# Row means from a ninth router column, variances from ACT's Square, and the states' sum as one bf16 product of exact pieces

## The chip, the core and the metric

The kernel runs on one core of a Trainium2 chip. The core has five engines with queues of their own: TensorE (PE; its weight loads are shown as PEld), VectorE (DVE), ScalarE (ACT), GpSimd (POOL) and SyncE (SP, which here only starts transfers). An engine works its queue in order, and semaphores make one engine wait for another. The metric is the device time in microseconds of one execution; the median of three runs of the kernel before is 476.83 us (476.71 to 477.4).

## The reference

One layer over 4096 tokens of width 256: a Mamba-like mixer with a residual and a layer norm, then a router that gives each token to one of eight feed-forward experts, again with a residual and a layer norm.

```python
xz = input_tensor @ W_in                       # 256 -> 1024
conv_in, gated = xz[..., :512], xz[..., 512:]
convolved = silu(causal_conv4(conv_in) + conv_b)
x_dbl = convolved @ W_x                        # 512 -> 33
delta = softplus(x_dbl[..., :1])
Bm, Cm = x_dbl[..., 1:17], x_dbl[..., 17:]
deltaA, deltaBx = exp(delta * -exp(A_log)), delta * Bm * convolved[..., :16]
# per token: h = dA * h + dBx ;  ys = sum(h * c) over the 16 states
skip_out = ys[..., None] + convolved * D_param
x1 = layernorm(x + (skip_out * silu(gated)) @ W_out)
e = argmax(x1 @ Wr.T + br)
out = layernorm(x1 + relu(x1 @ W1[e].T + b1[e]) @ W2[e].T + b2[e])
```

A layer norm takes the mean and the variance of each row of 256 and gives `(x - m) / sqrt(v + 1e-5)`. `ys` is one number per token, added to all 512 channels.

## The kernel before

The 4096 tokens go through the mixer in eight blocks of 512 (`NB`, `TB`). The loop over `k` (L1047) is a software pipeline: in one round it projects block k, works on the states of block k - 1, gates and projects out block k - 2, and ranks the tokens of block k - 3 for the experts. From round 6 on, quarters of expert blocks (`expert(n)`) are woven in, and after the loop the last rounds and the remaining expert blocks follow. There are 32 blocks of up to 128 tokens of one expert; from about 290 us on only these are left.

The order on TensorE is written out by hand (`manual_schedule` for PE, L120), and is that of the calls in the loop. The other engines' orders are set by a planner that goes by estimated times; so a change of one operation can move others of the same engine. An engine still works in order whatever the planner chose.

The pieces of a round that matter here, in TensorE's order:

- `project(k, c)`, c from 0 to 7 (L744): 128 channels by 512 tokens in fp32, two products of 128 rows each, which TensorE runs as four instructions, into one of three PSUM banks `mm`. ACT takes them out: channels 0 to 511 twice (a copy `xc`, L761, and `acc`, L763, the first tap of the convolution), the rest through Silu into `sg` (L759). VectorE does the other three taps (L723), ACT the Silu of the result, `cv` (L772).
- `gate(k - 2)` (L865), after `project(k, 0)`: the states times C, `hC`, are summed over the 16 states and spread over 128 partitions by a product with ones, `py` (L872). In fp32 this is done in two halves of 256 tokens, on rows 0 to 15 and 32 to 47 of the array, which run side by side into two banks. VectorE then forms `cv * D + py` (L879), eight times 128x256, and VectorE and POOL multiply by `sg` (L884).
- `gauge(k - 1)` and `gauge_out(k - 1)` (L780, L794): the 33 columns of `W_x`, turned so that tokens lie on partitions, and the step sizes `delta` by a series on VectorE, into `sr`.
- `project_out(k - 2, j)`, j from 0 to 3 (L916), spread over the round: 128 tokens by 256 + 8 columns, four products. The eight columns beside W_out are W_out times the router's weights (`router_behind`, L484), and `look` and `look_out` (L886, L901) add x times the router's weights, so that the router's sums come with the rows. The router's weights have their mean over the 256 features taken out first (`router_weights`, L470), so the logits need only the scale of the layer norm. VectorE adds the product to `xb` (L924) and takes the mean and the variance with its statistics instructions (L928, L929). After j = 3 ACT takes the square root (L934), VectorE the reciprocal and the offset `nma` (L935, L937), and ACT writes the normalized rows `x1` (L940), which a transfer stores for the experts.
- `scan(k - 1)` (L841), late in the round: `sr` is turned so that states lie on partitions (`pt`, L846), ACT forms the decay `dA` (L848), VectorE the input `dBx` (L850), the scan over 512 tokens (L852) and `hC` (L860). `hC` is then taken by `gate` of the next round. `sg` of projection 6 and the copies `rparts` (L912) stand in front of `dA` on ACT.
- `choose`, `rank`, `place` (L948, L974, L1014): argmax, rank of each token in its expert's list, and the lists as 0/1 products `pz` (L1019), which VectorE adds to `lists` (L1023).

ACT holds one set of function tables at a time; Silu, Exp and Sqrt are in different ones here, and a change shows in the profile as an ACT_TABLE_LOAD of 1283 ns.

Of the kernel before, what the change touches and what calls it, by code (L numbers as in the profile page):

```python
# [47 lines left out]
P = 128  # L48
# [37 lines left out]

O2 = DC * FF
# [12 lines left out]
def mamba_moe(  # L100
# [36 lines left out]
    def load(i):  # L137

        xTb = a2.tile([P, DC, TB], F32, tag="xTb", name=f"xTb{i}")
        at = slice(i * TB, (i + 1) * TB)  # L140
        if i:
            nc.sync.dma_start(xTb, xT[:, at].rearrange("(c p) t -> p c t", p=P))

        xb = a2.tile([P, JT, D + NE], F32, tag="xb", name=f"xb{i}")
        st[i] = {"xTb": xTb, "xb": xb}
# [29 lines left out]
    nc.vector.memset(wr, 0.0)  # L175
    nc.sync.dma_start(wr[:, :, 0:NE], WrT.rearrange("(c p) e -> p c e", p=P))
# [5 lines left out]
    wout = const.tile([P, CC, D + NE], F32, name="wout")  # L182
# [60 lines left out]
    nc.gpsimd.memset(sr, 0.0)  # L243
    ones8 = const.tile([P, NE], F32, name="ones8")
# [239 lines left out]
    def router_behind(half):  # L484
        po = bank("tr", f"pwo{half}", 2)
        pov = po[:, 0 : CC * NE].rearrange("p (c e) -> p c e", e=NE)
        cs = slice(half * CC // 2, (half + 1) * CC // 2)
        for c in range(CC)[cs]:
            for dc in range(DC):
                nc.tensor.matmul(  # L490
                    pov[:, c, :], lhsT=woutT[:, dc, c * P : (c + 1) * P], rhs=wr[:, dc, 0:NE],
                    start=(dc == 0), stop=(dc == DC - 1),
                )
        nc.scalar.copy(wout[:, cs, D : D + NE], pov[:, cs, :])
# [346 lines left out]
    def scan(i):  # L841
# [15 lines left out]
        hC = a2.tile([Q + NS, TB // 2], F32, tag="hC", name=f"hC{i}", bufs=1)  # L857
        for g in range(2):
            at = slice(g * TB // 2, (g + 1) * TB // 2)
            nc.vector.tensor_tensor(  # L860
                hC[g * Q : g * Q + NS, :], pt[RC : RC + NS, at], h[:, at], ALU.mult
            )
        s_["h"], s_["hC"] = h, hC

    def gate(i):  # L865
# [3 lines left out]
        pys = [bank("o", f"py{i}_{g}") for g in range(2)]  # L869
        for g, py in enumerate(pys):  # L870
            at = slice(g * Q, g * Q + NS)
            nc.tensor.matmul(  # L872
                py[:, 0 : TB // 2], lhsT=ones[at, :], rhs=st[i]["hC"][at, :], start=True,
                stop=True, tile_position=(g * Q, 0),
            )
        for c in range(CC):
            for g, py in enumerate(pys):
                at = slice(g * TB // 2, (g + 1) * TB // 2)
                nc.vector.scalar_tensor_tensor(  # L879
                    cv[:, c, at], cv[:, c, at], dp[:, c : c + 1], py[:, 0 : TB // 2],  # L880
                    ALU.mult, ALU.add,
                )
# [18 lines left out]
    def look_out(i):  # L901
# [7 lines left out]
        beside = st[i]["xb"][:, :, D : D + NE].rearrange("p (h s) e -> p h s e", s=2)  # L909
        parts = a2.tile([P, 2, DC, 2, NE], F32, tag="rparts", name=f"rparts{i}", bufs=1)  # L910
        for s in range(2):
            nc.scalar.copy(parts[:, s], pfv[:, s, :, :, 0:NE])  # L912
# [3 lines left out]
    def project_out(i, j):  # L916
        s_, sg, xb = st[i], st[i]["sg"], st[i]["xb"]
        po = bank("o", f"po{i}_{j}")
        for c in range(CC):
            nc.tensor.matmul(  # L920
                po[:, 0 : D + NE], lhsT=sg[:, c, j * P : (j + 1) * P], rhs=wout[:, c, :],
                start=(c == 0), stop=(c == CC - 1),
            )
        nc.vector.tensor_tensor(xb[:, j, :], po[:, 0 : D + NE], xb[:, j, :], ALU.add)  # L924
        if j == 0:
            s_["mv"] = a2.tile([P, JT, 2], F32, tag="mva", name=f"mva{i}")
        sta = a2.tile([P, 6], F32, tag="sta", name=f"sta{i}_{j}")
        nc.vector.bn_stats(sta, xb[:, j, 0:D])  # L928
        nc.vector.bn_aggr(s_["mv"][:, j, :], sta)  # L929
        if j < JT - 1:  # L930
            return
        mv = s_["mv"]
        sd = s_["sd"] = a2.tile([P, JT], F32, tag="sda", name=f"sda{i}")
        nc.scalar.activation(sd, mv[:, :, 1], AF.Sqrt, bias=eps)  # L934
        nc.vector.reciprocal(sd, sd)  # L935
        nm = a2.tile([P, JT], F32, tag="nma", name=f"nma{i}")
        nc.vector.scalar_tensor_tensor(nm, mv[:, :, 0], -1.0, sd, ALU.mult, ALU.mult)  # L937
# [269 lines left out]
```

## Time and profile before

| | |
|---|---|
| median of three runs | 476.83 us (476.71 to 477.4) |
| the profiled execution | 479.7 us, span 478.0 us |
| granted TensorE clock, mean | 0.993 |
| TensorE busy | 466.2 us, 98% of the span |
| weight loads | 350.1 us |
| VectorE busy | 340.4 us, 1120 instructions |
| ACT busy | 223.4 us, 453 instructions |
| POOL busy | 185.5 us, 194 instructions |
| VectorE in 97.5 to 125.0 us (one round) | 24.98 of 27.50 us |
| ACT in the same round | 21.65 us |

The page is one profiled execution. It gives busy times and their course over the span in 40 slices, in tenths. A group of instructions stands as line, engine, operation, out<-in, shapes, count, then busy time and mean duration, then the idle time of the engine in front of them and what ended it. Matmuls are pipelined, and the ends shown are modelled: a group of four fp32 projections of 512 columns shows 1.88 us, while the next one starts 1.72 us after it. So the starts tell how long TensorE's stream needs.

### The profile page before, as it was taken

Reading aid. Unit: us, or ns where it says so; the run is one execution under the profiler, and the core shown is the slowest. Engines: PE = TensorE matmul, PEld = TensorE weight load, DVE = VectorE, ACT = ScalarE, POOL = GpSimd, SP = SyncE. Lnnn points to the kernel's source line nnn. Section 1 sums busy time; section 2 is a strip of 40 time slices with the busy share of each in tenths; the row PEclk is TensorE's granted clock in tenths of the full one; section 3 lists DMA queues with packets and bytes.
Section 4 is the critical chain, followed back from the end, with each engine's and each line's share of the span. In section 5 each row is a group of like instructions: output and inputs, shape, how many; then the busy total and the mean of one; then the engine's idle time right before and its main releaser. Section 6 shows DMA issues by size and latency. Waiting matters only on the chain. (4 is left out here: it accounts for less than half of the span.)

```text
span 478.0 us, 7559 instructions
## 1 busy us (share of the span) xinstructions
PE 466.2 (98%) x2606; PEld 350.1 (73%) x2606; DVE 340.4 (71%) x1120; ACT 223.4 (47%) x453; POOL 185.5 (39%) x194
## 2 busy tenths in 40 slices
PE   8999999999999999999999999999999999999994
PEld 6444554645455566677788999999989898989884
DVE  1687959899898997986998978755446565645453
ACT  3776767886896877584625131212212121212111
POOL 2001203442418372450433423435445456654541
PEclk9998999999999999999999999999999999999998
DMA  8401012040124945250766759799997279977910
GB/s 237 166 1 45 0 42 91 1 132 0 47 87 149 431 159 188 110 199 18 271 242 225 270 209 366 260 368 350 359 347 277 60 253 345 313 247 245 353 44 22
DMA packets 23401, 89.98 MB, mean 188 GB/s; under 512 B 4914, under 2 KB 14909, under 8 KB 19650
## 3 DMA queue, kind: packets, MB, share of 16 engines
q0 software_dynamic: 8752, 74.71, 42.7%
q1 hardware_dynamic: 13650, 14.50, 9.3%
q8 instruction: 21, 0.34, 0.3%
q10 hardware_dynamic: 960, 0.27, 0.3%
q14 instruction: 18, 0.15, 0.1%
HBM read 87.78 MB, written 9.43 MB: 203 GB/s over the span
## 5 line engine op out<-in xcount | busy, mean ns | idle before, releaser
L744 PE MATMUL pm<-xTb,win 128*128 128x512 f32 (+1 forms) x264 | 122.5, 598 | 0.0
L587 PEld LDWEIGHTS ph<-xgT,we 128*128 128x128 f32 x864 | 100.8, 192 | 5.5 <-DVE r L637 1.3
L587 PE MATMUL ph<-xgT,we 128*128 128x128 f32 x864 | 103.0, 276 | 0.0
L612 PE MATMUL pe<-we,hT 128*128 128x256 f32 x432 | 98.9, 380 | 0.0
L612 PEld LDWEIGHTS pe<-we,hT 128*128 128x128 f32 x432 | 79.7, 190 | 10.0 <-DVE lg L960 0.3
L723 DVE SCALAR_TENSOR_TENSOR acc<-xc,cw,acc 128x512 f32<-128x512 f32 x96 | 72.6, 777 | 15.7 <-DMA wx<-in_W_x 8.6
L744 PEld LDWEIGHTS pm<-xTb,win 128*128 128x128 f32 x264 | 49.2, 195 | 45.5 <-issue 40.8
L262 ACT ACTIVATE sdm<-mvm,eps 128x1 f32<-128x1 f32 x32 | 9.4, 294 | 122.6 <-DVE mvm L260 116.8
L522 POOL DMA_INDIRECT we<-in_experts,widx x32 | 33.6, 1049 | 85.0 <-DVE r L637 24.9
L920 PE MATMUL po<-wout,sg 128*128 128x264 f32 x256 | 64.1, 392 | 1.0 <-DVE sg L884 0.9
L884 POOL TENSOR_TENSOR sg<-cv,sg 128x512 f32<-128x512 f32 x22 | 32.7, 1492 | 59.6 <-DVE cv L879 46.1
L920 PEld LDWEIGHTS po<-wout,sg 128*128 128x128 f32 x256 | 46.1, 190 | 11.0 <-issue 2.9
L650 POOL DMA_INDIRECT out<-y,tidx x32 | 32.9, 1027 | 38.5 <-DVE y L264 30.5
L598 DVE TENSOR_SCALAR hT<-ph,we 128x128 f32<-128x128 f32 x108 | 31.3, 341 | 20.7 <-PE ph L587 20.6
L637 DVE TENSOR_TENSOR r<-pe,xs 128x256 f32<-128x256 f32 x32 | 13.5, 422 | 43.9 <-PE pe L612 43.8
L504 POOL DMA_INDIRECT xg<-x1d,tidx x32 | 31.9, 998 | 29.7 <-DVE xd L810 7.5
L596 ACT ACTIVATE hT<-ph,we 128x128 f32<-128x128 f32 x108 | 30.8, 368 | 23.2 <-PE ph L587 20.7
L1008 POOL TENSOR_SCALAR rowh<-lrow,row,code 128x256 f16<-128x256 bf16 x20 | 26.0, 1307 | 27.9 <-DVE row L1000 26.7
L879 DVE SCALAR_TENSOR_TENSOR cv<-cv,dp,py 128x256 f32<-128x256 f32 x64 | 28.5, 469 | 3.4 <-PE py L872 3.4
L759 ACT ACTIVATE sg<-pm 128x512 f32<-128x512 f32 x32 | 19.1, 596 | 19.5 <-PE pm L744 17.0
L761 ACT COPY xc<-pm 128x512 f32<-128x512 f32 x32 | 18.6, 582 | 19.1 <-PE pm L744 18.8
L763 ACT ACTIVATE acc<-pm,cb,cw 128x512 f32<-128x512 f32 x32 | 25.1, 784 | 0.0
(219 smaller groups left out, 604.4 us busy)
## 6 DMA issues: line engine op xcount, KB each, us to landing
xb<-in_x SPq DMA_DIRECT2D x8, 512.0 KB, 6.1
x1d<-x SPq DMA_DIRECT2D x8, 512.0 KB, 4.8
xTb<-in_xT SPq DMA_DIRECT2D x7, 512.0 KB, 3.3
win<-in_W_in SPq DMA_DIRECT2D x1, 512.0 KB, 5.2
we<-in_W_outT SPq DMA_DIRECT2D x1, 512.0 KB, 5.9
wout<-in_W_out SPq DMA_DIRECT2D x1, 512.0 KB, 6.9
we<-in_experts,widx POOLq DMA_INDIRECT x32, 10.3
xg<-x1d,tidx POOLq DMA_INDIRECT x32, 6.6
```

Source lines behind the costliest of these rows:

```text
L504: nc.gpsimd.indirect_dma_start(out=to, out_offset=None, in_=x1d[0:rows, :], in_offset=bass.IndirectOffsetOnAxis(ap=at, axis=0),)
L522: nc.gpsimd.indirect_dma_start(out=wes[n][:, :], out_offset=None, in_=experts, in_offset=bass.IndirectOffsetOnAxis(ap=weights[n], axis=0), ...
L587: nc.tensor.matmul(ph[:, n * w : (n + 1) * w], lhsT=we[:, at : at + P], rhs=xgT[:, dc * w : (dc + 1) * w], start=(dc == 0), stop=(dc == DC ...
L596: nc.scalar.activation(hT[:, fc, :], ph[:, n * w : (n + 1) * w], AF.Relu, bias=bias)
L598: last[b] = nc.vector.tensor_scalar(hT[:, fc, :], ph[:, n * w : (n + 1) * w], bias, 0.0, ALU.add, ALU.max)
L612: nc.tensor.matmul(py[:, 0:D], lhsT=hT[:, fc, 0:P], rhs=out_weights(fc), start=(fc == 0), stop=(fc == FC - 1),)
L650: moved = nc.gpsimd.indirect_dma_start(out=out, out_offset=bass.IndirectOffsetOnAxis(ap=at, axis=0), in_=rows, in_offset=None, bounds_chec ...
L723: nc.vector.scalar_tensor_tensor(acc, xc[:, c, k : k + TB], cw[:, c, k : k + 1], acc, ALU.mult, ALU.add)
L744: nc.tensor.matmul(banks[c][:, at], lhsT=win[:, dc, c * P : (c + 1) * P], rhs=xTb[:, dc, at], start=(dc == 0), stop=(dc == DC - 1),)
L879: nc.vector.scalar_tensor_tensor(cv[:, c, at], cv[:, c, at], dp[:, c : c + 1], py[:, 0 : TB // 2], ALU.mult, ALU.add,)
L884: eng.tensor_tensor(sg[:, c, :], cv[:, c, :], sg[:, c, :], ALU.mult)
L920: nc.tensor.matmul(po[:, 0 : D + NE], lhsT=sg[:, c, j * P : (j + 1) * P], rhs=wout[:, c, :], start=(c == 0), stop=(c == CC - 1),)
```

## The change

Three edits.

The router's columns become nine: the ninth column of `wr` is set to -1/256, so that the ninth column beside W_out, and the ninth sum of `look`, give minus the mean of the row. With it the statistics instructions go. The squares of the row less its mean come from ACT's Square, with the ninth column as bias and the accumulator as output; Sqrt then scales their sum by 1/256. The offset is the ninth column times the reciprocal.

The product of the states is cut into bf16 pieces. VectorE multiplies the states and C into rows 0 to 15 of `parts_`, which is cleared once. It then subtracts from these their upper half-words, read as bf16, and writes the rest to rows 32 to 47, and the same once more to rows 64 to 79. The upper half-words of all 128 rows, every second bf16 of the tile, are the moving operand of one bf16 product with ones, of 512 columns, into one bank.

The gate's update is then four operations of 128x512 and no longer eight of 128x256.

```diff
+NM = NE + 1
-        xb = a2.tile([P, JT, D + NE], F32, tag="xb", name=f"xb{i}")
+        xb = a2.tile([P, JT, D + NM], F32, tag="xb", name=f"xb{i}")
     nc.vector.memset(wr, 0.0)
+    nc.vector.memset(wr[:, :, NE:NM], -1.0 / D)
-    wout = const.tile([P, CC, D + NE], F32, name="wout")
+    wout = const.tile([P, CC, D + NM], F32, name="wout")
+    parts_ = const.tile([P, TB], F32, name="parts_")
+    nc.gpsimd.memset(parts_, 0.0)
...
                 nc.tensor.matmul(
-                    pov[:, c, :], lhsT=woutT[:, dc, c * P : (c + 1) * P], rhs=wr[:, dc, 0:NE],
+                    pov[:, c, :], lhsT=woutT[:, dc, c * P : (c + 1) * P], rhs=wr[:, dc, 0:NM],
                     start=(dc == 0), stop=(dc == DC - 1),
                 )
-        nc.scalar.copy(wout[:, cs, D : D + NE], pov[:, cs, :])
+        nc.scalar.copy(wout[:, cs, D : D + NM], pov[:, cs, :])
...
-        hC = a2.tile([Q + NS, TB // 2], F32, tag="hC", name=f"hC{i}", bufs=1)
-        for g in range(2):
-            at = slice(g * TB // 2, (g + 1) * TB // 2)
+        s_["h"] = h
+        nc.vector.tensor_tensor(parts_[0:NS, :], pt[RC : RC + NS, :], h, ALU.mult)
+        for n in range(2):
+            this = slice(n * Q, n * Q + NS)
             nc.vector.tensor_tensor(
-                hC[g * Q : g * Q + NS, :], pt[RC : RC + NS, at], h[:, at], ALU.mult
-            )
-        s_["h"], s_["hC"] = h, hC
+                parts_[(n + 1) * Q : (n + 1) * Q + NS, :], parts_[this, :], upper(this),
+                ALU.subtract,
+            )
+
+    def upper(rows):
+        return parts_[rows, :].bitcast(BF16).rearrange("p (t two) -> p t two", two=2)[:, :, 1]
...
-        pys = [bank("o", f"py{i}_{g}") for g in range(2)]
-        for g, py in enumerate(pys):
-            at = slice(g * Q, g * Q + NS)
-            nc.tensor.matmul(
-                py[:, 0 : TB // 2], lhsT=ones[at, :], rhs=st[i]["hC"][at, :], start=True,
-                stop=True, tile_position=(g * Q, 0),
-            )
+        py = bank("o", f"py{i}")
+        nc.tensor.matmul(py, lhsT=oneb, rhs=upper(slice(0, P)), start=True, stop=True)
         for c in range(CC):
-            for g, py in enumerate(pys):
-                at = slice(g * TB // 2, (g + 1) * TB // 2)
-                nc.vector.scalar_tensor_tensor(
-                    cv[:, c, at], cv[:, c, at], dp[:, c : c + 1], py[:, 0 : TB // 2],
-                    ALU.mult, ALU.add,
-                )
+            nc.vector.scalar_tensor_tensor(
+                cv[:, c, :], cv[:, c, :], dp[:, c : c + 1], py, ALU.mult, ALU.add
+            )
...
-                po[:, 0 : D + NE], lhsT=sg[:, c, j * P : (j + 1) * P], rhs=wout[:, c, :],
+                po[:, 0 : D + NM], lhsT=sg[:, c, j * P : (j + 1) * P], rhs=wout[:, c, :],
...
-            s_["mv"] = a2.tile([P, JT, 2], F32, tag="mva", name=f"mva{i}")
-        sta = a2.tile([P, 6], F32, tag="sta", name=f"sta{i}_{j}")
-        nc.vector.bn_stats(sta, xb[:, j, 0:D])
-        nc.vector.bn_aggr(s_["mv"][:, j, :], sta)
+            s_["sq"] = a2.tile([P, JT], F32, tag="sqa", name=f"sqa{i}")
+        squares = a2.tile([P, D], F32, tag="sta", name=f"sta{i}_{j}")
+        nc.scalar.activation(
+            squares, xb[:, j, 0:D], AF.Square, bias=xb[:, j, D + NE : D + NM],
+            accum_out=s_["sq"][:, j : j + 1],
+        )
...
-        nc.scalar.activation(sd, mv[:, :, 1], AF.Sqrt, bias=eps)
+        nc.scalar.activation(sd, s_["sq"], AF.Sqrt, scale=1.0 / D, bias=eps)
         nc.vector.reciprocal(sd, sd)
         nm = a2.tile([P, JT], F32, tag="nma", name=f"nma{i}")
-        nc.vector.scalar_tensor_tensor(nm, mv[:, :, 0], -1.0, sd, ALU.mult, ALU.mult)
+        nc.vector.tensor_tensor(nm, xb[:, :, D + NE], sd, ALU.mult)
```

The sums of `look_out` (L909 to L914) get nine columns in the same way.

## The prediction

> **What bounds the kernel now.** I read the page first, part 1 for shares and part 2 for the course over the span:
>
> ```profile
> PE 466.2 (98%) x2606; PEld 350.1 (73%) x2606; DVE 340.4 (71%) x1120; ACT 223.4 (47%) x453; POOL 185.5 (39%) x194
> ...
> PE   8999999999999999999999999999999999999994
> ...
> DVE  1687959899898997986998978755446565645453
> ACT  3776767886896877584625131212212121212111
> ```
>
> TensorE is busy in every slice; VectorE is near full only up to about 190 us, where the eight token blocks go through the Mamba half, and ACT is at 60 to 90% there. So time moves only where TensorE's own stream gets shorter or where it is made to wait. Then the groups of instructions, for the operations that come and go:
>
> ```profile
> L940 ACT ACTIVATE x<-xb,nma,sda 128x256 f32<-128x256 f32 x32 | 16.6, 590 | 6.8 <-DVE nma L937 6.8
> ...
> L928 DVE BATCH_NORM_STATS2 sta<-xb 128x6 f32<-128x256 f32 x32 | 13.4, 418 | 0.3
> ...
> L860 DVE TENSOR_TENSOR hC<-pt,h 16x256 f32<-16x256 f32 x16 | 6.7, 419 | 0.5
> ...
> L872 PE MATMUL py<-hC,ones 16*128 16x256 f32 x32 | 6.4, 426 | 0.2 <-DVE hC L860 0.2
> ```
>
> Last the timeline around the states' sum `py` of block 3 (start, duration in us):
>
> ```profile
> 120.89 0.68 ACT L848 ACTIVATE dA<-pt,nega 16x512 f32<-16x512 f32 x1
> ...
> 121.25 0.43 DVE L924 TENSOR_TENSOR xb<-po,xb 128x264 f32<-128x264 f32 x1 [1.39 <-PE po L920]
> 121.72 0.68 DVE L850 TENSOR_TENSOR dBx<-pt,cv 16x512 f32<-16x512 f32 x1
> 122.33 0.41 DVE L928 BATCH_NORM_STATS2 sta<-xb 128x6 f32<-128x256 f32 x1
> ...
> 122.66 1.25 DVE L852 TENSOR_TENSOR_SCAN h<-dA,h,dBx 16x512 f32<-16x512 f32 x1
> 122.77 0.61 PE L1019 MATMUL pz<-colh,rowh 128*128 128x128 f16 x8
> ...
> 123.22 1.94 PE L744 MATMUL pm<-xTb,win 128*128 128x512 f32 x4
> ...
> 124.02 0.87 DVE L860 TENSOR_TENSOR hC<-pt,h 16x256 f32<-16x256 f32 x2
> 124.92 0.42 DVE L1023 TENSOR_TENSOR lists<-lists,pz 128x256 f32<-128x256 f32 x1
> ...
> 125.08 0.70 PE L872 MATMUL py<-hC,ones 16*128 16x256 f32 x4
> ...
> 125.71 0.70 PE L744 MATMUL pm<-xTb,win 128*128 128x512 f32 x1
> ```
>
> This decides the case. `py` stands in TensorE's fixed order between two projections. `hC` is done at 124.02 + 0.87 = 124.89 and TensorE takes it at 125.08: 0.19 us of slack. The chain before it begins with the decay `dA` (ACT, done at 121.57), before which VectorE was idle for 1.39 us, so a less loaded VectorE does not start it sooner. In blocks 0 and 1 TensorE already meets a late `hC`; in blocks 2 and 4 the slack is again 0.19 us (97.35 against 97.54, 151.99 against 152.18); in blocks 5 to 7 it is 7.6, 1.5 and 2.6 us.
>
> **The change, part by part.** The profiled execution took 479.7 us (span 478.0); the sum is made against it and then put on the median of 476.83.
>
> *The product on TensorE.* Starts tell more than busy times. From `pm` at 123.22 to the next tiled product at 127.63 are 4.41 us. Two projections take 2 x 1.72 (121.05 to 122.77 is one), and the switch to a tile of fewer columns and the short 16-bit `pz` in front add 0.15; so two fp32 pairs cost 4.41 - 3.44 - 0.15 = 0.82 us of stream. The new product is one pass of 512 columns over 2-byte values. The nearest row is `pz`: 8 products of 128 columns from 122.77 to 123.22, 0.056 each, so 0.22 for 512. But each value is read from every second half-word; the upper end is the fp32 instruction of 512 columns, 1.72 / 4 = 0.43. I take 0.22, by the 2-byte row. Saving: 0.60 per block, 0.4 where a tiled product follows (block 6).
>
> *The ninth column.* 256 `po` instructions go from 264 to 265 columns: at 1.72 / 4 / 512 = 0.84 ns per column, +0.2 us in all.
>
> *The chain to the product on VectorE.* It loses two multiplies of 419 ns and gains one of 512 columns and two subtractions. The multiply is like `dBx` (L850, PSUM and SBUF in, 682 ns); the subtractions like L884 on VectorE (two SBUF inputs, 710 ns mean, with some port sharing in it): 0.69 each. They depend on each other, about 0.035 us apart as `dBx`, scan and `hC` are in block 0 (40.65, 41.37, 42.62). The new order puts `lists` and the reciprocal between them. Block 3 by hand: `dBx` ends 122.40; with no statistics in the way the scan runs 122.44 to 123.69; multiply to 124.41; `lists` to 124.76; subtraction to 125.38; reciprocal to 125.41 on its own time (its Sqrt is done by about 124.0); subtraction to 126.11; `py` at 126.17 instead of 125.08. TensorE then resumes at 126.17 + 0.22 = 126.39 instead of 125.71, and its second weight load is no longer 0.10 late: +0.6. So the cheaper product starts 1.1 us later, and the block loses. Blocks 2 and 4 are the same, block 1 has no `lists`: +0.5. Block 0, with `dA` at 40.62 either way: scan to 42.58, multiply 43.30, subtractions 44.03 and 44.75, `py` 44.80 and projection at 45.02 against 44.17, less the weight load: +0.75. Sum of blocks 0 to 4: 0.75 + 0.5 + 3 x 0.6 = +3.05. Blocks 5 to 7 have slack for 1.1 us more and keep the saving: -0.6 - 0.4 - 0.6 = -1.6.
>
> *VectorE's load.* Per block 4 x (418 + 173) of statistics, 2 x 419, 8 gate updates of 469 and 480 for `nma` go; 2.06 of chain, 4 gate updates of 512 columns (L723 has 777 for that size; 469 less half its columns' 267 doubled gives 735) and a small `nma` come: 7.4 against 5.2, some 2.2 us less. Worth something only where TensorE waited on VectorE behind the gate:
>
> ```profile
> 108.38 0.71 PE L920 MATMUL po<-wout,sg 128*128 128x264 f32 x2 [0.95 <-DVE sg L884]
> ```
>
> By starts that wait is 1.1, and another at 134.99 is 0.2. In the new order the last gate product comes about 6.7 us after `py`, TensorE needs it 9.5 us after: -1.3. Elsewhere VectorE's gain is covered by TensorE's stream.
>
> *Squares on ACT.* 32 activations with a per-row bias and an accumulator. No row has one: below lies L772 without per-row operands (628 ns for 512 columns, so 415 for 256), above L940 with two (590) plus a small accumulator instruction of 0.2 like L816. I take 0.55, between them near L940: 17.6 us of work. Table loads fall from 49 to 45, 4 x 1.283 = -5.1. ACT goes from about 79% to 82% in blocks 2 to 5. What counts is what queues behind: three Squares stand ahead of `rx`, the eviction of projection 6 and hence `dA`, each waiting for its `xb` on VectorE. Before, ACT idled 2.13 us just there, waiting for TensorE; 3 x 0.55 fits into that, but the third Square needs an `xb` that was done only 0.2 us before the eviction began. Ends: 0, and the whole 1.65 per block. With VectorE's statistics gone from in front of that `xb` I take 0.3 in each of blocks 2 to 4: +0.9. In the expert phase the same order delays Relu evictions by up to 2 us; `close` comes two quarters later, so nothing.
>
> *The rest.* The memsets of `parts_` and of the ninth column run at the start, on engines that then wait for inputs: 0. The rows of `xb` are loaded an iteration early: 0.
>
> Sum: 3.05 - 1.6 + 0.2 - 1.3 + 0.9 = +1.25, so 479.7 becomes 480.95, and 476.83 becomes 478.1.
>
> **A rule against a row.** What the clock does with longer stalls shows in three stretches (columns: length, TensorE busy, ..., granted clock):
>
> ```profile
> 41.38:44.80 3.42, 3.23 (x16) 2.03 (x15) 3.02 (x6) 2.36 (x5) 0.00 (x0) 1.00 0.43 156
> 44.80:48.21 3.41, 3.41 (x8) 0.78 (x8) 3.41 (x6) 0.82 (x2) 2.35 (x2) 0.50 0.01 2
> 97.50:125.00 27.50, 26.55 (x108) 14.30 (x107) 24.98 (x72) 21.65 (x36) 10.52 (x8) 1.00 0.18 56
> ```
>
> After 3.4 us of eight-column products and the waits at `py` the clock was halved for 3.41 us, a loss of 1.7; a lone stall of 0.95 (at 107.4) cost none. New stalls of 1.1 amid full products are like the second: 0, and the upper end 4 x 1.7 = 6.8. The Trainium skill, TensorE: Matmul & The Clock Gate, "HAM oscillation", warns only of idle gaps above some 3.4 us; by that alone block 0 would not have been throttled, yet it was. By the rule the new stalls cost 0, by the row up to 6.8.
>
> **The rivals.**
> 1. *TensorE's saving is kept (other side).* If the states' pieces were ready when TensorE comes, all blocks save: -(7 x 0.6 + 0.4) + 0.2 - 1.3 = -5.7, so 471.1. It decides from 1.1 us of slack on; the chain hangs on `dA`, and 0.19 is measured, which speaks against it. Halfway (shorter subtractions, earlier `dA`): -2.
> 2. *ACT becomes the limit.* If a Square takes 0.8 and each block's `dA` slips by a full 1 us in four blocks: +1.25 - 0.9 + 4 = +4.4, so 481.2. For it: ACT's in-order queue, 22 of 27.5 us busy. Against: the 2.13 us of idle there.
> 3. *The clock falls.* One to four halvings on top: 479.8 to 484.9. For it block 0, against it the stall at 107.4.
> 4. *The product is no cheaper.* At 0.43 for the half-word reads: 8 x 0.21 = +1.7, so 479.8.
>
> **How the numbers follow.** A change below 0.2%, 0.95 us, can't be told from none here. Likeliest, the sum above: 0.47, own range 476.9 to 479.5. Rival 1 0.16, rival 2 0.20, rival 3 0.10, rival 4 0.07. Faster (below 475.9): rival 1, less its upper edge, 0.05 of the likeliest more: 0.20. Same (475.9 to 477.8): 0.17 of the likeliest and the edges: 0.22. Slower: 0.58. The range from 474.3 to 482.0 leaves out the full rival 1 and several halvings.
>
> **What would show it.** Right: `py` x8 of 512 columns, starting some 1.1 us after the preceding projection has ended in blocks 0 to 4, released by VectorE's second subtraction; no wait at `po` near 108; no statistics on VectorE; 45 table loads; TensorE busy about 5 us less and idle about 6 more. Wrong: TensorE idle at `mm` banks behind ACT, a second stretch at half clock, `py` at 0.43, or no wait at `py` at all, which would mean that `dA` came earlier.

## The result and the profile after

The changed kernel takes 483.54 us (median of four runs, 482.66 to 484.16), the kernel before 477.12 us beside it: ratio 1.0126, 95% interval 1.0099 to 1.0152. A second set of six runs gave 482.26 against 477.22, ratio 1.0105 (1.0078 to 1.0131). The forecast was 478.1 us with a range up to 482.0: the direction is right, the size is not. The profiled executions are 484.16 and 479.7 us long, spans 482.4 and 478.0: 4.4 us apart, less than the 6.4 us of the first medians. Part of that is TensorE's clock, which is halved for 3.4 us at a time in some runs of either kernel, the two profiled ones among them. In the second set (e5), with a mean clock of 0.996 or more the changed kernel took 481.1 to 481.5 us (three of six runs) and the kernel before 476.7 (median of 13 of 17); with 0.994 or less, 484.0 and 479.3 (medians). So the change costs 4.7 us between runs of like clock, and most of the rest is a matter of how many runs met a halved stretch.

The page of the changed kernel, parts 1 and 2:

```profile
PE 461.9 (96%) x2582; PEld 348.5 (72%) x2582; DVE 332.1 (69%) x1033; ACT 235.5 (49%) x513; POOL 186.9 (39%) x195
...
PE   8997999989898979999999999999999999999994
...
DVE  1677959698897957976988968844456465645453
ACT  3776687888977767585746242122122121212111
```

TensorE works 4.3 us less than before (466.2) and the span is 4.4 us longer, so it stands idle 8.7 us more; I had expected 5 less and 6 more. The slices of 8 and 7 in its row all lie in the mixer, up to about 190 us. The groups, with different shapes kept apart (`sta` is now the tile of the squares, `parts__145` the tile of the pieces):

```profile
L923 PE MATMUL po<-wout,sg 128*128 128x265 f32 x256 | 64.0, 392 | 0.0
...
L931 ACT ACTIVATE sta<-xb 128x256 f32<-128x256 f32 x32 | 16.2, 506 | 28.4 <-DVE xb L927 24.0 <-DVE row L412 4.2
...
L867 DVE TENSOR_TENSOR parts__145<-parts__145 16x512 f32<-16x512 f32 x16 | 10.9, 682 | 0.5
...
L931 ACT ACTIVATION_READ_ACCUMULATOR sta<-xb 128x1 f32 x32 | 6.0, 188 | 0.0
...
L864 DVE TENSOR_TENSOR parts__145<-pt,h 16x512 f32<-16x512 f32 x8 | 5.5, 685 | 0.3
...
L881 PE MATMUL py<-parts__145,oneb 128*128 128x512 bf16 x8 | 3.3, 407 | 8.6 <-DVE parts__145 L867 8.5
```

Three lines carry the reading. TensorE waits 8.6 us at eight products `py`, nearly all for VectorE's pieces (L867). It no longer waits at `po` (0.0). And ACT waits 28.4 us in front of its 32 Squares, which work only 16.2 + 6.0 us: in an in-order queue, everything behind a Square waits with it.

The table of TensorE's waits (total in us, times, longest) says where its idle time went. First the kernel before, then the changed one:

```profile
PE po L920 <- DVE sg L884: 0.9, 1, 0.9
...
PE pt L846 <- ACT rx L899: 0.7, 1, 0.7
...
PE py L872 <- DVE hC L860: 0.2, 1, 0.2
```

```profile
PE py L881 <- DVE parts__145 L867: 8.5, 5, 2.3
PE pt L852 <- ACT rx L902: 2.6, 2, 1.9
```

So 8.3 us of new wait at `py`, 1.9 us of new wait at the transposes `pt`, and 0.9 us less at `po`. The timeline around the product of block 3 (start, duration) answers to the one shown of before:

```profile
122.53 0.68 ACT L854 ACTIVATE dA<-pt,nega 16x512 f32<-16x512 f32 x1
...
122.89 0.43 DVE L927 TENSOR_TENSOR xb<-po,xb 128x265 f32<-128x265 f32 x1 [1.45 <-PE po L923]
...
123.36 0.68 DVE L856 TENSOR_TENSOR dBx<-pt,cv 16x512 f32<-16x512 f32 x1
...
124.08 1.27 DVE L858 TENSOR_TENSOR_SCAN h<-dA,h,dBx 16x512 f32<-16x512 f32 x1
...
124.86 1.94 PE L750 MATMUL pm<-xTb,win 128*128 128x512 f32 x4
...
125.38 0.69 DVE L864 TENSOR_TENSOR parts__145<-pt,h 16x512 f32<-16x512 f32 x1
...
126.10 0.42 DVE L1027 TENSOR_TENSOR lists<-lists,pz 128x256 f32<-128x256 f32 x1
...
126.55 0.68 DVE L867 TENSOR_TENSOR parts__145<-parts__145 16x512 f32<-16x512 f32 x1
...
127.47 0.68 DVE L867 TENSOR_TENSOR parts__145<-parts__145 16x512 f32<-16x512 f32 x1
...
128.21 0.39 PE L881 MATMUL py<-parts__145,oneb 128*128 128x512 bf16 x1 [1.41 <-DVE parts__145 L867]
...
128.43 1.02 PE L750 MATMUL pm<-xTb,win 128*128 128x512 f32 x2
```

The product starts at 128.21, and the next projection 0.22 us later, as forecast for two-byte values. But TensorE was free for it after 1.72 us of projection, at 126.6, and stood still until 128.21. From dA's end (123.21) the chain needs 5.00 us to `py`; before it was 3.51 us (121.57 to 125.08).

The other new wait is in block 5. Timeline of the changed kernel, 171 to 180 us:

```profile
173.10 0.22 DVE L843 TENSOR_TENSOR sr<-xd,sr 128x64 f32<-128x64 f32 x1
173.25 0.43 DVE L927 TENSOR_TENSOR xb<-po,xb 128x265 f32<-128x265 f32 x1
...
173.71 0.51 ACT L931 ACTIVATE sta<-xb 128x256 f32<-128x256 f32 x1 [4.14 <-DVE xb L927]
...
174.32 1.28 ACT L765 ACT_TABLE_LOAD   x1
...
178.12 0.37 ACT L902 COPY rx<-prx 128x256 f32<-128x256 f32 x1
...
178.54 0.64 PE L852 MATMUL pt<-ident,sr 128*80 128x128 f32 x4 [1.93 <-ACT rx L902]
...
179.70 0.44 PE L561 MATMUL pg<-ident,xg 128*128 128x128 f32 x2 [0.52 <-ACT rparts L915]
```

VectorE adds the first rows of block 4 (`xb`) only at 173.25, behind the taps and the series for `sr`. The Square of these rows stands at the head of ACT's queue and waits 4.14 us; then come a table load, four Silus (`sg` and `cv` twice), a second Square, and only at 178.12 the eviction `rx`. (`prx` holds the sums of `look`, and `rx` is ACT's copy of them.) It frees the PSUM bank that `pt` of block 5 needs, so TensorE waits, although `sr`, which `pt` reads, was done at 173.32. In the kernel before, in the same round, ACT took `rx` 6.6 us earlier and `pt` started without a wait:

```profile
171.49 0.37 ACT L899 COPY rx<-prx 128x256 f32<-128x256 f32 x1
...
172.71 0.60 PE L846 MATMUL pt<-ident,sr 128*80 128x128 f32 x4
```

For the experiments I use one more measure, since the runs of the kernel before spread by 8 us in some sets: the length of **seven rounds**, from the start of `px` (the first product of `gauge`) of block 0 to that of block 7 in the profile, less 1.7 us where the halved clock lies in it. It is 202.65 us before (24.36 to 228.71, less 1.7) and 207.45 us for the changed kernel (24.68 to 233.83, less 1.7). The changed kernel profiled once more on another chip (e5) gives 207.46, so the measure repeats far better than the medians. Round by round, against the forecast for the same round (the ninth column's 0.2 left out):

| round, from px to px | before | after | difference | forecast |
|---|---|---|---|---|
| 0 to 1 (product of block 0) | 21.69 | 22.48 | +0.79 | +0.75 |
| 1 to 2 | 25.95 | 26.68 | +0.73 | +0.5 |
| 2 to 3 | 26.38 | 27.35 | +0.97 | +0.9 |
| 3 to 4 | 27.55 | 27.35 | -0.20 | -0.2 |
| 4 to 5 | 27.10 | 28.20 | +1.10 | +0.7 |
| 5 to 6 | 36.79 | 38.29 | +1.50 | -0.6 |
| 6 to 7 | 37.19 | 37.10 | -0.09 | -0.4 |
| px of block 7 to the last pz | 68.37 | 67.88 | -0.49 | -0.6 |

The sum is +4.3 us; the inputs came 0.3 us later and the expert blocks took 0.2 us less, which makes the span's 4.4. Of the 3.3 us by which these rounds miss the forecast, 2.1 are in one of them.

### The profile page after: what moved, and what is told of

It is laid out like the page before. It is cut to its first block, busy times and chain, and to the rows that moved or that the text cites. A ratio compares the mean times of both kernels' runs of the same rounds, so it can differ in the third digit from the quotient of the medians.

```text
span 482.4 us, 7503 instructions
## 1 busy us (share of the span) xinstructions
PE 461.9 (96%) x2582; PEld 348.5 (72%) x2582; DVE 332.1 (69%) x1033; ACT 235.5 (49%) x513; POOL 186.9 (39%) x195
## 4 chain that ended last, share of the span: by engine, by line
PE 77%; DVE 14%; ACT 4%; issue 3%; DMA 1%; POOL 0%; POOLq 0%; SPq 0%; ACTq 0%
PE ph L593 24%; PE pe L618 21%; PE pm L750 14%; PE po L923 10%; DVE acc L729 4%; PE px L793 2%; DVE parts__145 L867 2%; DVE h L858 2%; PE pg L561 1%; PE pf L629 1%; DVE cv L883 1%; DVE dBx L856 1%; DVE parts__145 L864 1%; DVE xb L927 1%; DMA win<-in_W_in 1%
## 5 line engine op out<-in xcount | busy, mean ns | idle before, releaser
L923 PE MATMUL po<-wout,sg 128*128 128x265 f32 x256 | 64.0, 392 | 0.0
L887 POOL TENSOR_TENSOR sg<-cv,sg 128x512 f32<-128x512 f32 x22 | 29.3, 1357 | 62.9 <-DVE cv L883 59.6
L931 ACT ACTIVATE sta<-xb 128x256 f32<-128x256 f32 x32 | 16.2, 506 | 28.4 <-DVE xb L927 24.0
L883 DVE SCALAR_TENSOR_TENSOR cv<-cv,dp,py 128x512 f32<-128x512 f32 x32 | 23.5, 738 | 0.9 <-PE py L881 0.8
```

The costliest lines, as they stand in the source:

```text
L883: nc.vector.scalar_tensor_tensor(cv[:, c, :], cv[:, c, :], dp[:, c : c + 1], py, ALU.mult, ALU.add)
L887: eng.tensor_tensor(sg[:, c, :], cv[:, c, :], sg[:, c, :], ALU.mult)
L923: nc.tensor.matmul(po[:, 0 : D + NM], lhsT=sg[:, c, j * P : (j + 1) * P], rhs=wout[:, c, :], start=(c == 0), stop=(c == CC - 1),)
```

## The experiments

Two theories had to be told apart. A: the chain of pieces on VectorE holds up the product in blocks 0 to 4. B: the Squares in ACT's queue hold up `rx` and `dA`. Rivals: the halved clock, and a loss in the product itself. Every set ran beside the kernel before, whose median is given; ratios are to it.

**Each part alone.** e1 has the pieces, the single product and the four gate updates, with statistics and eight columns as before; e2 has the ninth column and the Squares, with `hC` and the two fp32 halves.

```diff
 # e1: on the kernel before
-        hC = a2.tile([Q + NS, TB // 2], F32, ...)
+        nc.vector.tensor_tensor(parts_[0:NS, :], pt[RC : RC + NS, :], h, ALU.mult)
...
 # e2: on the changed kernel
-        nc.vector.tensor_tensor(parts_[0:NS, :], pt[RC : RC + NS, :], h, ALU.mult)
+        hC = a2.tile([Q + NS, TB // 2], F32, ...)
...
```

> The kernel before with the states' sum alone changed: the pieces, one 16-bit product of 512 columns, four gate updates. Statistics and eight router columns as before. Theory A (the chain of pieces on VectorE delays the product in blocks 0 to 4): the product starts about 1.1 us later there and is 0.60 shorter, in blocks 5 to 7 the saving is kept; in the changed kernel blocks 0 to 4 showed +0.98, +0.64, +0.97, -0.19 and +1.08, so 2 to 4 us slower than before, 479 to 481. Theory B (the loss comes from the Squares in ACT's queue alone): at or below before, 474 to 477.

> The kernel before with the statistics alone changed: ninth column, Squares on ACT; the states' sum in fp32 halves as before. Theory B (Squares wait on VectorE in ACT's queue, in front of the eviction rx and of dA): the stall of about 2.1 us at the transposes of block 5 and up to 1 us in block 4 are there, +0.2 for the columns, the stall at the gated product near 108 may shrink by 1.1: 2 to 3.5 us slower, 479 to 480.6. Theory A alone: within 1 us of before, since the chain to the product is the old one. If A and B simply add up, the losses of this run and of the pieces alone together give the 6.4 us of the whole change.

Measured: e1 488.66 us, ratio 1.0106 (1.0059 to 1.0152); e2 489.03, ratio 1.0110 (1.0071 to 1.0149); before 484.91. Seven rounds: e1 207.15 (+4.5), e2 204.94 (+2.3). The medians show the two alike because e2's six runs have mean clocks of 0.985 to 0.993 and e1's 0.994 to 0.999. Both theories hold. The waits of TensorE that count, in e1 and in e2:

```profile
PE py L877 <- DVE parts__144 L863: 8.2, 6, 1.9
```

```profile
PE pt L850 <- ACT rx L903: 3.6, 2, 2.9
```

The wait at `pt` was 0.7 us before; the 2.9 are in block 5. The two losses make 6.8 us and the whole change has 4.8. The excess lies in two rounds. In round 4 to 5, e1, which keeps VectorE's statistics, waits 1.3 us at `prx` for the rank (`rk`), which the changed kernel does not. In round 5 to 6, e2 waits 2.9 us at `pt` and the changed kernel 1.9. The wait at `po` is gone in e1 and in e2: either half of the change takes it away.

**The Squares out of the way.** e3 issues all four Squares of a block behind `dA` of the same round; e12 does so in one round only, that of block 4.

```diff
-        nc.scalar.activation(dA, pt[RD : RD + NS, :], AF.Exp, scale=nega)
+        s_["dA"] = nc.scalar.activation(dA, pt[RD : RD + NS, :], AF.Exp, scale=nega)
...
-        nc.scalar.activation(squares, xb[:, j, 0:D], AF.Square, ...)
+        if j < JT - 1 and i + 1 < NB:     # e12: and i == 4
+            return
+        for n in range(JT):
+            with tc.issue_after(st[i + 1]["dA"].ins):
+                nc.scalar.activation(squares, xb[:, n, 0:D], AF.Square, ...)
```

> The changed kernel, but in every block with a scan in its round all four Squares are issued on ACT behind dA, so that none of them stands in front of rx or dA. Theory B: the stall at the transposes of block 5 goes (2.1 us) and dA of block 4 is 1 us earlier: 2 to 3 us faster than the changed kernel, 480.5 to 481.5. Theory A alone: as the changed kernel, 483 to 484. Against it: four more table loads, and the normalized rows come some 2 us later, which in blocks 0 to 6 nobody waits for.

> The changed kernel with the four Squares of block 4 alone put behind dA of block 5; all the other Squares stay. If the one Square that waited 4.14 us on xb in front of rx makes the stall before the transposes of block 5, that stall (2.1 us) and the 0.3 at the turned rows behind it go, and nothing else does: 2.4 us less up to the end of the mixer than the changed kernel, 1.005 of before in all. If the stall comes of something else (VectorE late with sr, the bank), it stays, 1.010.

Measured: e3 485.78 us, ratio 1.0031 (1.0000 to 1.0062), seven rounds 203.86, 3.6 us less than the changed kernel, somewhat more than the 2 to 3 expected. e12 482.64 us, ratio 1.0087 (1.0060 to 1.0114), seven rounds 205.02, 2.4 us less than the changed kernel, as expected. The round 5 to 6 of e12 takes 35.85 us and no longer 38.29, and its `pt` of block 5 starts with no wait recorded:

```profile
173.63 0.60 ACT L765 ACTIVATE sg<-pm 128x512 f32<-128x512 f32 x1 [2.90 <-PE pm L750]
173.65 0.60 PE L852 MATMUL pt<-ident,sr 128*80 128x128 f32 x4
```

Now ACT waits there for TensorE. So the Squares of one block, two of them in front of `rx`, cost 2.4 us in one round; the other 1.2 us that e3 gains come from the other rounds. What is left in e3 against the kernel before, 1.2 us, is the chain: 6.8 us of wait at `py`.

**The chain's length.** e7 and e8 are e3 with one subtraction and with none. They sum two pieces and one; the third, or the second and the third, are left out of the states' sum.

```diff
-        for n in range(2):
+        for n in range(1):                # e7; e8 has no loop at all
             this = slice(n * Q, n * Q + NS)
             nc.vector.tensor_tensor(parts_[(n + 1) * Q : ...], parts_[this, :], upper(this), ALU.subtract)
```

> The kernel with the Squares behind dA, one subtraction less: the product sums two pieces, the third is left out (about 16 bits of the product's 24 remain). Theory A: the wait of TensorE at the product falls by one subtraction, 0.72 us, in each of blocks 0 to 4 (1.73, 1.43, 1.37, 1.37, 1.37 us become 1.01, 0.71, 0.65, 0.65, 0.65): 3.6 us less up to the end of the mixer. If another thing than the chain holds TensorE there (the weight load, the cost of a 16-bit product), less than 1 us.

> The same with no subtraction: the product sums the upper half-words of the states times C alone, the two other pieces are left out. Theory A: the waits of 1.37 to 1.73 us at the product in blocks 0 to 4 fall by 1.42 each, to 0.3 or less: 6.5 to 7 us less up to the end of the mixer than with three pieces, and less time than the kernel before. If VectorE's next work is as late anyway (the gate's updates wait at the gated product instead), 2 to 4 us less.

Measured: e7 474.67 us, ratio 0.9942 (0.9923 to 0.9961); e8 470.96, ratio 0.9870 (0.9846 to 0.9894); before 477.22.

| kernel | subtractions | wait at py, total | seven rounds |
|---|---|---|---|
| e3 | 2 | 6.8 | 203.86 |
| e7 | 1 | 3.2 | 199.86 |
| e8 | 0 | 0.5 | 196.49 |

Each subtraction left out takes 3.4 to 4.0 us off, on average 0.7 to 0.8 per block of the first five; its own length on VectorE is 0.68. Theory A is shown, with its price. Without the subtractions the product of 0.22 us is worth what it promised: e8 is 6.3 us faster than the kernel before by the medians, and in seven rounds 4.9 us less than e6 below, which has the Squares in the same place and the fp32 halves.

**The product later in TensorE's order.** If the pieces are 1.6 us late, TensorE could do another projection first.

```diff
         project(k, 0)
-        if have(b):
-            gate(b)
         expert(fill[0])
         project(k, 1)
+        if have(b):
+            gate(b)
```

> The changed kernel with the states' product one projection later in TensorE's order (after projection 1 of the round, no longer after projection 0), which gives the chain on VectorE 1.72 us more. Theory A: the waits at the product in blocks 0 to 4 (about 1.1 us each) go, 4 to 6 us faster than the changed kernel, 477.5 to 479.5; the gate products come at the same time, and TensorE wants them where it did. Theory B alone: as the changed kernel, 483 to 484. Rival C (a halved clock after idle gaps of TensorE): where the gaps go the halved stretch near 45 us goes too, 1.7 us more.

Measured: 496.88 us, ratio 1.0299 (1.0258 to 1.0341), seven rounds 211.5 (two halved stretches lie in them, so less 3.4), far off what was expected. The wait at `py` went as A says, but a larger one came further on. TensorE's waits in e4:

```profile
PE po L923 <- DVE sg L887: 8.7, 5, 3.0
PE pt L852 <- ACT rx L902: 2.8, 2, 2.1
...
PE po L923 <- POOL sg L887: 1.8, 4, 0.9
...
PE py L881 <- DVE parts__145 L867: 0.5, 1, 0.5
```

The gate's updates and products on VectorE and POOL follow `py`, and in the new order VectorE's planner put six taps (5.49 us) in front of the last gate product of block 1, so that `po` waited 3.0 us for it. The slack that I had counted behind the gate (9.5 us of TensorE against 6.7 of VectorE) held only for the order of VectorE's queue that I had counted it in.

**The Squares without the pieces.** e6 is e3 with `hC` and fp32 halves.

> Ninth column and Squares, all four Squares behind dA, and the states' sum in two fp32 halves as before (no pieces). If the Squares cost time only by standing in front of rx and dA, this has neither loss: the product starts where it did (0.5 us after the projection in front of it in blocks 0 to 4), there is no stall at the transposes of block 5, and the wait at the gated product near 108 us (1.1 us) is gone with VectorE's statistics: 1 to 2 us faster than before. If the Squares themselves or the later normalized rows cost something, 0 to 2 us slower than before.

Measured: 477.37 us, ratio 0.9995 (0.9971 to 1.0020), seven rounds 201.4, 1.2 us less than before. The product starts 0.5 us after the projection's last instruction as before, and the wait at `po` falls from 0.9 to 0.2. So behind `dA` the statistics on ACT cost nothing and bring about a microsecond in seven rounds. That gain is not seen in the medians.

**Starting the chain earlier.** In e3 VectorE is idle for 1.5 us before the fourth addition to `xb` (L927) with `dBx` and the scan queued behind it. e9 puts that addition behind `dBx`; e10 also puts the addition to `lists` behind the last subtraction; e11 is e9's edit on the kernel before.

```diff
-        nc.vector.tensor_tensor(xb[:, j, :], po[:, 0 : D + NM], xb[:, j, :], ALU.add)
+        with tc.issue_after(st[i + 1]["dBx"].ins) if j == JT - 1 and i + 1 < NB else ExitStack():
+            nc.vector.tensor_tensor(xb[:, j, :], po[:, 0 : D + NM], xb[:, j, :], ALU.add)
...
-        nc.vector.tensor_tensor(lists, lists, pz[:, 0 : LH * P], ALU.add)
+        with tc.issue_after(st[i + 2]["whole"].ins) if i + 2 < NB else ExitStack():      # e10
+            nc.vector.tensor_tensor(lists, lists, pz[:, 0 : LH * P], ALU.add)
```

> Three pieces, Squares behind dA, and on VectorE the addition of the fourth gated product (xb, row block 3) put behind dBx, which needs nothing of it. With the Squares behind dA alone, VectorE stood idle for 1.5 us before that addition, with dBx and the scan queued behind it, while dA was done 0.94 us before the scan began. If it is this order that makes the pieces late, the scan starts 0.73 us earlier in blocks 1 to 4, the wait at the product falls from 1.37 to 0.64 us there, 2.9 us in all: about 0.995 of the kernel before. If dA or the length of the chain itself is what counts, no change: 1.000 to 1.003 of before.

> The same, and the addition to the lists (0.42 us on VectorE, between the pieces in blocks 2 to 4) put behind the last subtraction. Another 0.45 us in three blocks, 1.3 us in all: about 0.992 of the kernel before, with a wait at the product of 0.2 us in blocks 2 to 4. If the other engines' work between the pieces is not on the path, as the run with dBx first alone.

> The control: the kernel before, with the addition of the fourth gated product behind dBx and nothing else. There TensorE finds hC ready 0.19 us before it comes in blocks 2 to 4, so an earlier scan is worth nothing at the product: 0.997 to 1.001 of the kernel before. If this is as fast as the pieces with the same order, the order alone is the gain, and the pieces bring nothing.

Measured, beside 476.77 us: e9 478.84, ratio 1.0049 (1.0026 to 1.0071); e10 477.60, 1.0020 (1.0000 to 1.0040); e11 479.02, 1.0027 (1.0004 to 1.0050). e9 missed: the scan did not start earlier. Its timeline in block 3:

```profile
121.64 0.68 ACT L854 ACTIVATE dA<-pt,nega 16x512 f32<-16x512 f32 x1
...
122.35 0.68 DVE L856 TENSOR_TENSOR dBx<-pt,cv 16x512 f32<-16x512 f32 x1 [1.79 <-ACT dA L854]
...
123.07 0.43 DVE L929 TENSOR_TENSOR xb<-po,xb 128x265 f32<-128x265 f32 x1
...
123.42 1.26 DVE L858 TENSOR_TENSOR_SCAN h<-dA,h,dBx 16x512 f32<-16x512 f32 x1
```

`dBx` has nothing of `dA`, and yet it waits until `dA` has ended. Both read the transposed states in one PSUM bank, and the program orders these two readers as they are written: `dA` first. e10 gains 1.3 us in seven rounds over e9 (203.2 against 204.5), as expected for `lists`. In e11 seven rounds take 201.9, 0.8 us less than before, but its runs met the halved clock more often (7 of 12 at 0.994 or less, against 8 of the 35 of the kernel before), which its median shows.

e13 and e14 are e9 and e10 with the call for `dBx` written ahead of that for `dA`; e15 is the same order on the kernel before, and e17 is e15 once more.

```diff
+        s_["dBx"] = nc.vector.tensor_tensor(dBx, pt[RB : RB + NS, :], cv[0:NS, 0, :], ALU.mult)
         nc.scalar.activation(dA, pt[RD : RD + NS, :], AF.Exp, scale=nega)
-        nc.vector.tensor_tensor(dBx, pt[RB : RB + NS, :], cv[0:NS, 0, :], ALU.mult)
```

> Three pieces, Squares behind dA, dBx ahead of the fourth addition on VectorE and ahead of dA in the order of the two readers of the transposed states, so that dBx waits for the transposes alone. The scan can then start when dA is done: about 0.7 us earlier in blocks 0 to 4 than with the Squares behind dA alone, the waits at the product become 1.0, 0.7, 0.65, 0.65 and 0.65 us, 3.6 us less up to the end of the mixer: 0.993 to 0.996 of the kernel before. If the length of the chain alone counts, no change: 1.002 to 1.005.

> The same with the addition to the lists behind the last subtraction: another 0.45 us in blocks 2 to 4, 1.3 us in all: 0.990 to 0.993 of the kernel before.

> The control: the kernel before with the same order of dBx. Its product already finds hC ready (0.19 us before TensorE comes) in blocks 2 to 4, so an earlier scan gains nothing there: 0.998 to 1.002 of the kernel before. If it gains as much as the three pieces with this order, the pieces bring nothing of their own.

> The kernel before with dBx ahead of dA and of the fourth addition, once more, on the chip of the next run. Up to the end of the mixer it was 2.6 us shorter than the kernel before without the halved stretch: 0.993 to 0.996 of the kernel before.

Now `dBx` runs while ACT loads its tables. e13 in block 3:

```profile
117.49 0.68 DVE L854 TENSOR_TENSOR dBx<-pt,cv 16x512 f32<-16x512 f32 x1 [0.45 <-PE pt L852]
...
118.72 0.68 ACT L856 ACTIVATE dA<-pt,nega 16x512 f32<-16x512 f32 x1
...
119.28 0.43 DVE L929 TENSOR_TENSOR xb<-po,xb 128x265 f32<-128x265 f32 x1 [1.01 <-PE po L923]
...
119.63 1.26 DVE L858 TENSOR_TENSOR_SCAN h<-dA,h,dBx 16x512 f32<-16x512 f32 x1
```

The scan starts 0.23 us after `dA`, not 0.94. Measured, beside 483.94 us: e13 482.27, ratio 0.9964 (0.9928 to 1.0001); e14 481.80, 0.9966 (0.9931 to 1.0001); e15 480.01, 0.9928 (0.9891 to 0.9966). e17 gave 481.17 against 483.13, ratio 0.9974 (0.9939 to 1.0009). Seven rounds: e13 200.40, e14 200.10, e15 199.49, e17 199.46. For e13 that is 3.5 us less than e3, as expected. But the control missed: the kernel before gains as much from this order (3.2 us). I had counted only the product in blocks 2 to 4. The gain lies in the first two rounds (0.7 and 0.3), where `hC` came late before, in round 3 to 4 (1.2), where the wait at `po` is gone, and in round 4 to 5 (0.7), where a wait of 0.4 at `prx` is gone. And in e14, where the wait at `py` is 1.6 us, all of it in blocks 0 and 1, the pieces are still no faster than the fp32 halves. TensorE's waits in e14 name the reason (`pxs` is ACT's copy of `px`, `pxo` its transposes):

```profile
PE py L881 <- DVE parts__145 L867: 1.6, 2, 1.2
PE pxo L806 <- ACT pxs L798: 1.5, 3, 0.5
```

The Squares behind `dA` make the normalized rows late, and ACT waits for their offset (1.22 us at 127.41) in front of `pxs`.

**Order and Squares together.** e18 is e15's order with ninth column and Squares behind `dA`, without pieces.

> The same order, with the ninth column and the Squares behind dA in place of VectorE's statistics, the states' sum in fp32 halves. The Squares behind dA alone gave 1.1 us up to the end of the mixer, by taking the wait at the gated product near 108 us; the order takes that wait too. If both act on the same wait, this is as fast as the order alone within 0.5 us (0.993 to 0.997); if they add up, 1 us faster (0.991 to 0.994).

Measured: 481.38 us beside 483.13, ratio 0.9963 (0.9928 to 0.9997), seven rounds 199.94. That is the order alone within 0.5 us, which fits that both act on the same wait. It is also the control for e13 and e14, with the same Squares and order but fp32 halves: 199.94 against 200.40 and 200.10, and it has neither of e14's two waits. By seven rounds the shortest kernel here that computes the whole sum is e15, the kernel before with two operations put in another order: 3.2 us less in both of its profiles, 0.993 and 0.997 of the time in two sets, the second with an interval that reaches 1.

**The gap filled.** e16 lets TensorE transpose the identity during its wait at `py`.

```diff
+        for n in range(12 if i < 5 else 0):
+            nc.tensor.transpose(py[:, n % 4 * P : (n % 4 + 1) * P], ident, ident)
         nc.tensor.matmul(py, lhsT=oneb, rhs=upper(slice(0, P)), start=True, stop=True)
```

> The changed kernel with twelve transposes of the identity (0.11 us each, 1.3 us) in front of the product in blocks 0 to 4, into its own bank, so that TensorE works through most of its wait there; the product starts when it did. If the idle gap in block 0 brings the halved stretch near 45 us, no run of this kernel shows it (mean clock 0.996 or more in all six), and its median is 1 to 1.5 us lower than the changed kernel's, 1.007 to 1.009 of before. If the halving is not caused by the gap, a third to a half of the runs still show 0.993 or less, and the time is the changed kernel's, 1.010.

Measured: 488.76 us beside 483.94, ratio 1.0106 (1.0055 to 1.0158); mean clocks of its six runs 0.986 to 0.996, of the kernel before in that set 0.989 to 0.999. The profiled run has no halved stretch near 45 us and one near 157 us. That one follows block 4, where the product came 1.5 us later after its projection than in the changed kernel, and TensorE still waited 2.4 us behind the transposes. So the gap of block 0 was filled, but the medians can't tell what that was worth; a cure it was not.

## Why the prediction was right and wrong

**What failed: the term "Squares on ACT".** I took +0.3 in each of blocks 2 to 4 and wrote that in the expert phase the order "delays Relu evictions by up to 2 us; `close` comes two quarters later, so nothing". For blocks 2 to 4 I had named `rx` and `dA` as standing behind the Squares, but bounded the loss by the Squares' work, 1.65 us per block. For the expert phase I looked at who waits for the Relus, and not at the other instructions behind the Square in the same queue. In round 6 one of them is `rx`, whose bank `pt` needs. That is the 2.1 us of round 5 to 6 (e12: 2.4 with what follows). In block 4 a Square's wait of 2.15 us in front of `dA` made `dA` start 3.03 us after the transposes, not 2.06 as before, where I had 0.3. In all, the Squares' place in the queue cost 3.6 us in seven rounds (the changed kernel against e3); the term was 0.9. A Square's work was sized well enough: I had 0.55 us, and four in a row start 0.49 us apart in e12. What counts is its wait for `xb`, 4.14 us in the worst case, and that is set by where VectorE's planner puts the addition. ACT works only 235.5 of 482.4 us; it did not run full, it stood in line.

**The chain was right, with small misses.** Blocks 0, 2 and 3 come out within 0.1 us (+0.79, +0.97, -0.20 against +0.75, +0.9, -0.2), block 1 0.2 higher. These forecasts have the Squares' 0.3 in them; e3, where the Squares are out of the way, has +0.79, +0.53, +0.76 and +0.58 in the rounds of blocks 0, 1, 2 and 4, where the chain alone was forecast at 0.75, 0.5, 0.6 and 0.6. In block 3 the chain from `dA` to `py` took 5.00 us, and by hand I had 4.60: from the multiply's end, the addition to `lists` and the two subtractions took 2.08 us and not 1.70. e7 and e8 show the mechanism with its price of 0.7 us per subtraction and block. The product's 0.22 us is exact, so rival 4 (no cheaper product) is out.

**The saving of blocks 5 to 7 was half right.** Round 6 to 7 and the stretch behind it together have -0.58 where I had -1.0; block 5's saving is there but buried under the new wait.

**The vanishing waits at `po`** (-1.3) are right: 0.9 us before, 0.0 after, and round 3 to 4 comes out as forecast. The reason that I gave, a VectorE with less to do, was only one way to it: the wait is also gone in e11, where nothing but VectorE's order changed.

**The rivals.** Rival 1 (the saving is kept) fell with 8.5 us of wait at `py`; e14 shows that even with the pieces nearly on time nothing is left of it, and e8 what it would have been. Rival 2 (ACT becomes the limit) was nearest in kind, 481.2 us, but named the wrong mark: I looked for a TensorE that stands at the `mm` banks behind ACT, and it stood at `pt`, behind `rx` in ACT's queue. That its price is close to the 481.1 to 481.5 us of the runs at the higher clock is luck: `dA` slipped by 1 us in one block and not in four, and most of the rest went elsewhere. Rival 3 (the clock falls) accounts for most of the 1.7 us by which the first 6.4 us exceed the 4.7 between runs of like clock.

**The rule and the row on the clock.** In the profiles of both kernels one stretch of the mixer has half the clock. In the changed kernel, this stretch and the one of the same length just ahead of it (columns: length, TensorE busy, ..., granted clock):

```profile
45.30:48.70 3.40, 3.40 (x5) 1.09 (x4) 3.37 (x5) 0.00 (x0) 1.98 (x2) 0.51 0.01 2
...
41.81:45.22 3.41, 1.51 (x11) 1.15 (x10) 3.27 (x5) 2.26 (x5) 0.00 (x0) 1.00 0.49 153
```

Both kernels pay the same 1.7 us in the profile, so the new stalls cost 0 there, the lower end. The Trainium skill, TensorE: Matmul & The Clock Gate, "HAM oscillation", warns of idle gaps above some 3.4 us; no wait of TensorE in the mixer of any kernel here reached that (the longest was 3.0), and the clock fell all the same. The next section of that page, "A second HAM failure mode: psum-queue depth-cycling", tells of a kernel whose clock oscillated through frequent short idles; I had passed over it, and the stretch ahead of 44.8 us in the kernel before, with products of eight columns and idle times below 1 us, is nearer to that.

The traces say more than I had read from them. In each of them the halved stretches begin a whole number of steps of 3.413 us after the first record of full clock (7.25 and 44.80 us in the kernel before: 11 steps). Of the 17 halved stretches in these traces, without those that reach the span's end, 14 follow a step in which TensorE was busy for 1.5 us or less, the products of eight or nine columns (`router_behind`) left out; the other three, in the kernel before, e6 and e11, follow one of 2.4 us. All 12 steps with 1.4 us or less (from 20 us after the start to 12 us before the end) were followed by half the clock, and of five with 1.44 to 1.49 us two. This points not to the longest wait but to how little TensorE does within one step, and that depends on where the steps lie, which differs from run to run. The wait of 1.90 us in block 0 falls within one step in the changed kernel (the second row above), with half the clock after it; in e12 the same 1.90 us are cut by the end of a step at 42.85 us, and the clock stays full. This is read from the traces; no run here tested it.

## What to carry to other kernels

Price a new instruction in an in-order queue not by its work alone but by how long it may wait and by who stands behind it: list everything queued behind it in each round, the evictions that free a bank first of all. A faster product on the busiest engine can be worth nothing if the work that prepares it goes onto the chain that TensorE already waits for; here each 0.68 us of it cost some 0.7 us in each of five blocks. Before lengthening such a chain, see what it starts behind: two operations put in another order in the old kernel brought 3.2 us in seven rounds, where the change lost 4.8.

## What the runs showed of the hardware

- A bf16 moving operand that takes every second half-word of an fp32 tile ran at the rate of the 16-bit product `pz` (0.056 us for 128 columns): 0.22 us for 512.
- ACT's accumulator is an instruction of its own, 0.188 us behind each Square of 0.506 us for 128x256; in e12, Squares that each have one follow each other 0.49 us apart.
- Two engines that read different rows of one PSUM bank were kept in the order of the program: `dBx` on VectorE waited 1.79 us for `dA` on ACT (e9), and 0.45 us for the transposes alone when it was written first (e13). The wait is one that the program carries, not one that the engines need for their data. The Trainium skill, PSUM — Partial Sum Buffer, "PSUM bank collisions raise a hardware error", says that two engines must not access one bank at once, reads included, and that accesses in different quarters of the partitions are exempt: `dA` reads rows 0 to 15 and `dBx` rows 32 to 47, so by it they could overlap. No run here tried that.
- The clock was halved for 3.41 us at a time in some runs of most of these kernels, 1.7 us of work lost each time. In the traces 14 of 17 such stretches follow a step of 3.41 us in which TensorE was busy for 1.5 us or less (products of eight or nine columns left out); the same wait cut by the end of a step left the clock full (e12).
